# A sparse attention layer on one core: where the residual rows of the last tiles are put in order, who adds their output bias, and how the last projections are spread

## The chip, the cores and the metric

The kernel runs on one core of a Trainium2 chip. The metric is the device time of one launch in microseconds; before the change it is 2045.74 us, the median of three runs from 2043.18 to 2046.87. The profiled execution took 2043.34 us and has a span of 2041.5 us from its first to its last instruction. Times inside a trace count from the start of that span.

## The reference

One layer of attention over a graph, with a residual and a normalisation, in float32. x is 16 x 1024 x 512, adj a 1024 x 1024 matrix of zeros and ones shared by all batches and heads; there are 8 heads of 64.

```python
q = (x @ Wq + bq).reshape(b, n, H, HD)          # k and v alike
scores = jnp.einsum('bqhd,bkhd->bhqk', q, k) / jnp.sqrt(jnp.float32(HD))
scores = scores + (1.0 - adj)[None, None, :, :] * -1000000000.0
attn = jax.nn.softmax(scores, axis=-1)
out = jnp.einsum('bhqk,bkhd->bqhd', attn, v).reshape(b, n, d) @ Wo + bo
y = x + out
y = (y - mean(y)) / sqrt(var(y) + 1e-5)          # over the last axis
```

The random adj has few ones in a row (about four in the mean, many in the first rows and few in the last), so nearly all scores are masked.

## The kernel before, in words

The kernel computes scores for existing edges alone. It first counts the ones of each row of adj, sorts the 1024 queries by that count (`ranks`), and writes lists of edges (`edges`, L412): for tile t of 128 sorted queries, OWN[t] rounds in which each query meets one key of its own, and for the two densest tiles BLOCKS[t] further rounds in which a query with many keys takes several rows. A round is called a block: 35 per batch, 560 in all. `asked_row` holds the sorted order of the queries; whatever belongs to a sorted tile (its q rows, its residual rows of x, its output rows) is gathered or scattered by an indirect DMA on GpSimd (POOL) with it.

*Fronts.* For each batch and each pair of tiles of x, `pair` (L564) transposes x and multiplies by Wq, Wk and Wv (for k and v of two tiles together it uses a scheme with seven half products, L666). q, k and v go to DRAM rows by plain DMAs on the SP queue, and so does the row of the mean of v (L615), after which the batch counts as `set_up`. All of a batch's rows must be there before its blocks are gathered. The temporary tiles of this scheme are t1 to t4, e, w and g.

*Blocks.* For block n, `gather` (L788) fetches kv rows (L810), and where needed q rows (L794, L804); `products` (L827, DVE) and `scores` (L831, DVE) give the scores, `exponentials` (L841, ACT) their exponentials, `weigh` multiplies v (eight ACT instructions at L851, or DVE at L855), `add_own` (L867, DVE) or `add_up` (L876, L877, PE) sums. At the end of a tile `normalise` (L879) divides, PE transposes the result (L902) and ACT copies it (L906).

*Finish.* `load_y` (L719) gathers the tile's residual rows of x; `finish` (L736) multiplies by Wo (PE, four products of 512 columns, each two weight loads and two matmuls in the trace) and then, one or two loop steps apart: DVE adds the residual (L743) and the bias with a running sum (L744); DVE centres (L747); ACT squares (L751); DVE finishes the variance (L754); POOL takes the power -1/2 (L757); DVE makes the shift (L760); ACT normalises (L763); POOL scatters the rows to the output (L767).

The order of all this is written out by hand: one Python loop (L982 to L1053) over steps n from -34 (LEAD_IN) until all is done lays the instructions down, and each engine executes its own in that order. Step n works at different depths on different blocks: it lays products for block n + 4, exponentials for n + 3, sums for n, and gathers up to block n + 8, or n + 11 once no front is left. `later(k, fn)` lays something k steps further on, `later_last` does so at the end of that step. The lists are built by generators that advance once per step, from step -18 on (EDGES_FROM). On PE each step may spend a `share` of time, in which a product counts 0.86 (PRODUCT), four transposes 0.44 (TRANSPOSE), a sum 0.87 (SUM):

- in the lead-in (n < 0) 3.45 per step (LEAD_SHARE);
- for n from 0, set anew every 35 steps so that the fronts keep a fixed distance ahead of the blocks (EARLY = 13 blocks, and FIRST = 9 more in the first batch);
- from the end of batch 12 on, what is left of the fronts divided by the steps up to `fronts_end`, L977: (16 - 1) x 35 - 13 - 3 = 509;
- after the last front 3.0 (LAST_SHARE).

Tiles 102 to 111 (SPILL; tile 8 b + t) don't finish at once: their attention results go to DRAM and come back (`reload`, L730) once no front is left, to give PE work in the last stretch. Their residual rows are loaded into the temporaries t1 to t4 of the fronts, those of all other tiles into six buffers named y. At the end `guard` sets a flag that selects a general path for other inputs (`tile_general`); it isn't run here.

Of the kernel before, what the change touches and what calls it, by code (L numbers as in the profile page):

```python
# [32 lines left out]
LAZY = 2  # L33

SPILL = range(102, 112)
AHEAD_LAST = 11

ROWS = 3
EARLY = 13

FIRST = 9
LEAD_IN = 34
EDGES_FROM = (-17, -16, -15, -13, -11, -8, -7, -18)

# [1 line left out]
SUM = 0.87  # L46
TRANSPOSE = 0.44
LEAD_SHARE = 3.45
LAST_SHARE = 3.0

P = 128
# [103 lines left out]
def kernel(  # L155
# [66 lines left out]
    with ExitStack() as main:  # L222
# [49 lines left out]
        out_views = dram_disjoint_views(out, B * NT)  # L272
        x_rows = x.rearrange("b n d -> (b n) d")
        spill = [dram.tile([P, D], F32, name=f"spill_{i}") for i in range(len(SPILL))]
        zero = work.tile([1, D], F32, tag="q", name="zero", bufs=2)
        nc.gpsimd.memset(zero, 0.0)
        bias_rows = one.tile([2 * NPAIR, P], F32, name="bias_rows")
# [62 lines left out]
        def later(k, fn):  # L340
            plan.setdefault(now[0] + k, []).append(fn)
# [374 lines left out]

        loaded = {}

        def load_y(b, t, k=None):  # L719
            if k is None:  # L720
                Y[b, t] = work.tile([P, D], F32, tag="y", name=f"y_{b}_{t}", bufs=Y_BUFS)
            else:
                Y[b, t] = work.tile([P, 2, D], F32, tag=f"t{k % 4 + 1}", name=f"y_{b}_{t}", bufs=1)[:, 0, :]
            loaded[b, t] = now[0]
            nc.gpsimd.indirect_dma_start(  # L725
                out=Y[b, t], out_offset=None, in_=x_rows,
                in_offset=bass.IndirectOffsetOnAxis(ap=asked_row[:, t:t + 1], axis=0), element_offset=b * N * D,
            )

        def reload(b, t, k):  # L730
            OT[b, t] = work.tile([P, D], F32, tag="ewg"[k % 3], name=f"oTs_{b}_{t}", bufs=1)
# [3 lines left out]

        def finish(b, t):  # L736

            def out(p):
                OT.pop((b, t))
                y = Y[b, t]  # L740

                st = small.tile([P, 5], F32, name="stats", bufs=6)
                nc.vector.tensor_tensor(y, p, y, op=OP.add)  # L743
                nc.vector.scalar_tensor_tensor(y, bo_bc, 1.0, y, op0=OP.mult, op1=OP.add, accum_out=st[:, 0:1])  # L744

                def centre():
                    nc.vector.tensor_scalar(st[:, 1:2], st[:, 0:1], -1.0 / D, None, op0=OP.mult)  # L747

                def spread():
                    sq = work.tile([P, D], F32, tag="ysq", name=f"ysq_{b}_{t}", bufs=1)  # L750
                    nc.scalar.activation(sq, y, AF.Square, bias=st[:, 1:2], accum_out=st[:, 2:3])  # L751

                def variance():
                    nc.vector.tensor_scalar(st[:, 2:3], st[:, 2:3], 1.0 / D, EPS, op0=OP.mult, op1=OP.add)  # L754

                def power():
                    nc.gpsimd.tensor_tensor(st[:, 3:4], st[:, 2:3], neg_half, op=OP.pow)  # L757

                def shift():
                    nc.vector.tensor_tensor(st[:, 4:5], st[:, 3:4], st[:, 1:2], op=OP.mult)  # L760

                def norm_out():
                    nc.scalar.activation(y, y, AF.Identity, bias=st[:, 4:5], scale=st[:, 3:4])  # L763
                    later(2, store)

                def store():
                    nc.gpsimd.indirect_dma_start(  # L767
                        out=out_rows[b, t], out_offset=bass.IndirectOffsetOnAxis(ap=asked_row[:, t:t + 1], axis=0),
                        in_=y, in_offset=None, element_offset=b * N * D,
                    )  # L770
                    del Y[b, t]

                later(1, centre)
                later_last(2, spread)
                later(3, variance)
                later(4, power)
                later(5, shift)
                later_last(6, norm_out)

            return product(f"po_{b}_{t}", lambda: OT[b, t], W["o"], out)  # L780

# [184 lines left out]
        with tc.manual_schedule():  # L968

            fronts += transpose_x(0, 0) + transpose_x(0, 1)  # L970
            for b in range(B):
                for j in range(NT // 2):
                    fronts += pair(b, j)
            fronts_time = sum(u[0] for u in fronts)
            batch_time = fronts_time / B
            finishing, last_finish, reloads, last_reload = [], -LEAD_IN, 0, 0
            fronts_end = (B - 1) * NB - EARLY - 3  # L977
            credit = 0.0
            for t in range(3):
                load_x(0, t)  # L980
            n = -LEAD_IN
            while n < total or plan or rest or urgent or done or finishing or spilled:  # L982
                now[0] = n
                if n < 0:
                    share = LEAD_SHARE if n > -LEAD_IN else TRANSPOSE * 1.5
                elif n >= SPILL[0] // NT * NB + NB:

                    share = sum(u[0] for u in fronts) / max(fronts_end - n, 1) + NS * SUM / NB if fronts else LAST_SHARE
                elif n % NB == 0:

                    left = sum(u[0] for u in fronts)
                    goal = fronts_time - (n // NB + 2 + (EARLY + (FIRST if n < NB else 0)) / NB) * batch_time
                    share = (max(0.0, left - goal) + NT * NPAIR * PRODUCT + NS * SUM) / NB
                if 0 <= n + 3 < total:
                    exponentials(n + 3)
                if 0 <= n + 4 < total:
                    products(n + 4)
                while gathered[0] < min(n + (AHEAD if fronts else AHEAD_LAST) + 1, total) and blocks[gathered[0]][0] in set_up:
                    gather(gathered[0])
                    gathered[0] += 1  # L1000
                if 0 <= n + 1 < total and not by_act(n + 1):
                    weigh(n + 1)
                if 0 <= n < total and blocks[n][2] < OWN[blocks[n][1]]:
                    add_own(n)
                if 0 <= n + 4 < total:
                    scores(n + 4)
                if 1 <= n <= total and (n == total or blocks[n][2] == 0):
                    normalise(*blocks[n - 1][:2])
                for fn in plan.pop(n, ()):
                    fn()  # L1010
                if 0 <= n + 2 < total and by_act(n + 2):
                    weigh(n + 2)
                for fn in rest.pop(n, ()):
                    fn()
                credit += share
                if 0 <= n < total and blocks[n][2] >= OWN[blocks[n][1]]:
                    add_up(n)
                    credit -= SUM
                for tile_done in done[:0 if fronts and len(done) < LAZY else 1 if fronts else 2] + coming:
                    if tile_done not in loaded and sum(b * NT + t not in SPILL for b, t in Y) < 5:  # L1020
                        load_y(*tile_done)
                coming[:] = [t for t in coming if t not in loaded]
                if spilled and not fronts and n > last_reload + 2 and sum(b * NT + t in SPILL for b, t in Y) < 3:
                    reload(*spilled.pop(0), reloads)
                    reloads, last_reload = reloads + 1, n
                first_unit = True
                while credit > 0 or urgent:
                    if urgent and not (first_unit and fronts):
                        urgent.pop(0)()
                        continue  # L1030
                    if not finishing and len(done) > (LAZY if fronts else 0) and n > loaded.get(done[0], n) + 1 and n > last_finish + 1:
                        finishing = finish(*done.pop(0))
                        last_finish = n
                    units = finishing or fronts
                    if not units:
                        if urgent:
                            urgent.pop(0)()
                            continue
                        break
                    cost, fn, ready = units[0]  # L1040
                    if ready and not ready():
                        if urgent:
                            urgent.pop(0)()
                            continue
                        break
                    del units[0]
                    fn()
                    credit -= cost
                    first_unit = False
                credit = min(credit, share)  # L1050
                preps += prep.pop(n, [])
                preps = [g for g in preps if next(g, True) is None]
                n += 1  # L1053

    word = nc.values_load(  # L1055
# [32 lines left out]
```

## Time and profile before

| engine | busy us of the span | share |
|---|---|---|
| PE (TensorE) | 1917.2 | 94% |
| DVE (VectorE) | 1801.0 | 88% |
| ACT (ScalarE) | 1684.6 | 83% |
| POOL (GpSimd) | 1302.5 | 64% |

Three quarters of the DMA time belongs to the queue of indirect DMAs that POOL issues: 59.8% of the time of 16 DMA engines, against 18.4% for the plain transfers of SP. Three groups of indirect DMAs have one instruction per tile: the output rows (L767, 128 times, 1180 ns of POOL each), the residual rows (L725, 128 times, 1117 ns) and the q rows (L794, 128 times, 1097 ns); the kv rows (L810) have 560.

How to read it: a busy share over the whole span is a mean over stages with different limits. The page's second part cuts the span in 40 slices of 51 us, one digit of tenths each, and shows where an engine is full. A view of windows gives the same for chosen stretches in microseconds, with the clock granted to PE. A group line gives a source line, the engine, what it writes and reads, how often, busy time and mean duration, and after the second bar the engine's idle time just before these instructions with what ended it; "issue" there means that no other engine was waited for. PE's matmuls overlap in the records, so the spacing of its weight loads (PEld) tells its pace better than its busy time.

### The profile page before, as it was taken

The page shows a single profiled execution, that of the slowest core. Times are in us where ns is not written, and L with a number is a line of the kernel's source. Part 1 is how long each engine was busy: PE and PEld are TensorE (multiplying, and loading weights), DVE is VectorE, ACT ScalarE, POOL GpSimd, SP SyncE. Part 2 cuts the span into 40 slices and gives each one's busy share as a digit, 9 for nine tenths or more (in the row PEclk, how much of TensorE's full clock was granted, in tenths as well). Part 3 has the DMA queues.
Part 4 walks back from the last instruction along what each step waited for, and adds up shares of the span by engine and source line. Part 5 has one row for each costly group of instructions (what it writes and reads, how often), then busy time and mean ns, then how long its engine had stood idle before and what let it go on. Part 6 is the DMA issues. An engine that isn't in the chain of part 4 may idle for free. (4 is left out here: it accounts for less than half of the span.)

```text
span 2041.5 us, 26505 instructions
## 1 busy us (share of the span) xinstructions
PE 1917.2 (94%) x5334; PEld 925.4 (45%) x5334; DVE 1801.0 (88%) x3675; ACT 1684.6 (83%) x7048; POOL 1302.5 (64%) x1224
## 2 busy tenths in 40 slices
PE   8979999899999999999999999999999999997565
PEld 4434454444545444444544444454544444443232
DVE  3798889889999989989999999989999999997684
ACT  4627879888897988889897989879798889987684
POOL 1432557757576666757676676758677675757884
PEclk9999999999999999999999999999999999999897
DMA  6565787878888787878888797888888799978773
GB/s 244 154 202 195 241 297 264 296 237 303 288 295 292 261 307 258 310 242 303 293 287 307 242 327 250 293 283 289 293 271 305 257 321 313 326 255 281 231 253 103
DMA packets 183657, 549.50 MB, mean 269 GB/s; under 512 B 30879, under 2 KB 30907, under 8 KB 183486
## 3 DMA queue, kind: packets, MB, share of 16 engines
q0 software_dynamic: 121632, 403.22, 59.8%
q1 hardware_dynamic: 59248, 139.53, 18.4%
q10 hardware_dynamic: 2606, 4.99, 0.7%
q14 instruction: 127, 1.04, 0.2%
q8 instruction: 44, 0.72, 0.1%
HBM read 435.44 MB, written 136.89 MB: 280 GB/s over the span
## 5 line engine op out<-in xcount | busy, mean ns | idle before, releaser
L810 POOL DMA_INDIRECT kvg<-kv_rows,key_row x560 | 634.9, 1134 | 468.1 <-ACT pv L841 145.1
L851 ACT ACTIVATE pv<-kvg,pv 128x64 f32<-128x64 f32 x3608 | 910.2, 342 | 0.0
L550 PE MATMUL pq<-wq,xT 128*128 128x512 f32 x1024 | 479.7, 599 | 0.2 <-DVE g L685 0.2
L550 PE MATMUL po<-wo,oT 128*128 128x512 f32 x944 | 439.0, 599 | 0.7 <-ACT oT L906 0.7
L831 DVE TENSOR_REDUCE s<-qk 128x8 f32<-128x512 f32 x560 | 381.0, 680 | 6.4
L827 DVE TENSOR_TENSOR qk<-qt,kvg 128x512 f32<-128x512 f32 x464 | 317.4, 684 | 5.9 <-DMA kvg<-kv_rows,key_row 5.8
L550 PEld LDWEIGHTS pq<-wq,xT 128*128 128x128 f32 x1024 | 193.8, 192 | 216.2 <-issue 197.4
L550 PEld LDWEIGHTS po<-wo,oT 128*128 128x128 f32 x944 | 176.5, 192 | 209.2 <-issue 191.8
L666 PE MATMUL x<-b,xT 128*128 128x512 f32 x504 | 239.1, 597 | 0.0
L666 PE MATMUL pp<-t,s 128*128 128x512 f32 x504 | 237.0, 592 | 0.4 <-DVE s L536 0.4
L867 DVE TENSOR_TENSOR pv<-pv,pv 128x520 f32<-128x520 f32 x336 | 233.1, 694 | 0.2 <-ACT pv L851 0.2
L841 ACT ACTIVATE pv<-s,absent 128x8 f32<-128x8 f32 x464 | 136.9, 296 | 85.1 <-DVE s L831 55.8
L767 POOL DMA_INDIRECT out_dram<-y,asked_row x128 | 151.0, 1180 | 35.5 <-issue 16.9
L725 POOL DMA_INDIRECT y<-in_x_dram,asked_row x128 | 143.0, 1117 | 38.9 <-issue 37.7
L562 ACT ACTIVATE sq<-q 128x128 f32<-128x128 f32 x512 | 151.1, 303 | 17.5 <-DVE q L577 17.1
L794 POOL DMA_INDIRECT qt<-q_rows,asked_row x128 | 140.4, 1097 | 38.9 <-issue 34.6
L562 ACT ACTIVATE sq<-kv 128x128 f32<-128x128 f32 x512 | 151.0, 302 | 0.1
L666 PEld LDWEIGHTS x<-b,xT 128*128 128x128 f32 x504 | 95.8, 191 | 116.6 <-issue 111.5
L666 PEld LDWEIGHTS pp<-t,s 128*128 128x128 f32 x504 | 94.8, 190 | 110.6 <-issue 99.2
L902 PE MATMUL poT<-ident,o 128*128 128x128 f32 x512 | 79.5, 279 | 50.2 <-DVE o L894 34.1
L666 PE MATMUL z<-b,s 128*128 128x512 f32 x252 | 120.1, 599 | 5.0 <-DVE kv L694 5.0
L804 POOL DMA_INDIRECT qg<-q_rows,query_row x96 | 106.9, 1114 | 27.8 <-issue 24.1
(168 smaller groups left out, 2816.1 us busy)
## 6 DMA issues: line engine op xcount, KB each, us to landing
kv_rows<-kv SPq DMA_DIRECT2D x128, 512.0 KB
x<-in_x_dram SPq DMA_DIRECT2D x128, 256.0 KB
q_rows<-q SPq DMA_DIRECT2D x128, 256.0 KB
kvg<-kv_rows,key_row POOLq DMA_INDIRECT x560, 5.8
adj<-in_adj_dram POOLq DMA_DIRECT2D x8, 512.0 KB, 12.7
spill<-oT SPq DMA_DIRECT2D x10, 256.0 KB
oTs<-spill SPq DMA_DIRECT2D x10, 256.0 KB
qt<-q_rows,asked_row POOLq DMA_INDIRECT x128, 5.0
```

The lines of the kernel that those rows point to most:

```text
L550: nc.tensor.matmul(p, lhs()[:, ts(c, P)], w[:, c, :], start=(c == 0), stop=(c == NPAIR - 1))
L562: nc.scalar.activation(sq, s[:, ts(h, P)], AF.Square, accum_out=NRM[b][:, i, t, h:h + 1])
L666: nc.tensor.matmul(R[bank], l[:, ts(c, P)], right[:, c, :], start=(first and c == 0), stop=(c == 1), skip_group_check=True,)
L725: nc.gpsimd.indirect_dma_start(out=Y[b, t], out_offset=None, in_=x_rows, in_offset=bass.IndirectOffsetOnAxis(ap=asked_row[:, t:t + 1], axi ...
L767: nc.gpsimd.indirect_dma_start(out=out_rows[b, t], out_offset=bass.IndirectOffsetOnAxis(ap=asked_row[:, t:t + 1], axis=0), in_=y, in_offse ...
L794: nc.gpsimd.indirect_dma_start(out=QT[b, t], out_offset=None, in_=q_rows[b % ROWS], in_offset=bass.IndirectOffsetOnAxis(ap=asked_row[:, t: ...
L810: nc.gpsimd.indirect_dma_start(out=KG[n], out_offset=None, in_=kv_rows[b % ROWS], in_offset=bass.IndirectOffsetOnAxis(ap=key_row[:, g:g + ...
L827: nc.vector.tensor_tensor(QK[n], q, KG[n][:, 0:D], op=OP.mult)
L831: nc.vector.tensor_reduce(S[n], QK.pop(n).rearrange("p (h d) -> p h d", d=HD), axis=AX.X, op=OP.add)
L841: nc.scalar.activation(PV[n][:, D:], S.pop(n), AF.Exp, bias=bias)
L851: nc.scalar.activation(pv[:, ts(h, HD)], v[:, ds(D + h * HD, HD)], AF.Copy, scale=pv[:, D + h:D + h + 1])
L867: nc.vector.tensor_tensor(PV[b, t], PV[b, t], pv, op=OP.add)
```

## The change

It does three things.

1. *Residual put in order early.* While the lists are built (steps -16 to -4, SORTED_AT, two tiles a step), POOL gathers the residual rows of the last 26 tiles (102 to 127) and SP writes them to DRAM in sorted order (`sort_residual`). When such a tile finishes, `load_y` takes it by a plain DMA on SP in place of an indirect one on POOL. It takes 26 indirect DMAs out of POOL's queue near the end.
2. *Bias on PE.* For tiles whose finish starts after the last front, the output bias is added in PSUM by one more product (a column of the identity, broadcast, times `bo_bc`), so that DVE's first addition falls away and the second takes PSUM and residual together. The shift and what follows it move one step later for these tiles.
3. *Fronts spread otherwise.* In the lead-in the share from step -16 on is 4.6 in place of 3.45 (LISTS_SHARE); in the first batch the fronts run 11 in place of 9 blocks further ahead (FIRST); and the last front is due at step (16 - 1) x 35 - 12 = 513 in place of 509, nearer to the blocks of the last batch, which need it.

```diff
--- before.py
+++ after.py
@@ -33,12 +33,14 @@
 LAZY = 2
 
 SPILL = range(102, 112)
+
+SORTED_AT = range(-16, -3)
 AHEAD_LAST = 11
 
 ROWS = 3
 EARLY = 13
 
-FIRST = 9
+FIRST = 11
 LEAD_IN = 34
 EDGES_FROM = (-17, -16, -15, -13, -11, -8, -7, -18)
 
@@ -46,6 +48,7 @@
 SUM = 0.87
 TRANSPOSE = 0.44
 LEAD_SHARE = 3.45
+LISTS_SHARE = 4.6
 LAST_SHARE = 3.0
 
 P = 128
@@ -272,6 +275,7 @@
         out_views = dram_disjoint_views(out, B * NT)
         x_rows = x.rearrange("b n d -> (b n) d")
         spill = [dram.tile([P, D], F32, name=f"spill_{i}") for i in range(len(SPILL))]
+        residual = [dram.tile([P, D], F32, name=f"residual_{i}") for i in range(B * NT - SPILL[0])]
         zero = work.tile([1, D], F32, tag="q", name="zero", bufs=2)
         nc.gpsimd.memset(zero, 0.0)
         bias_rows = one.tile([2 * NPAIR, P], F32, name="bias_rows")
@@ -716,16 +720,27 @@
 
         loaded = {}
 
+        def gather_x(y, b, t):
+            nc.gpsimd.indirect_dma_start(
+                out=y, out_offset=None, in_=x_rows,
+                in_offset=bass.IndirectOffsetOnAxis(ap=asked_row[:, t:t + 1], axis=0), element_offset=b * N * D,
+            )
+
+        def sort_residual(i):
+            y = work.tile([P, D], F32, tag="y", name=f"y_sorted_{i}", bufs=Y_BUFS)
+            gather_x(y, *divmod(SPILL[0] + i, NT))
+            later(2, lambda: nc.sync.dma_start(residual[i], y))
+
         def load_y(b, t, k=None):
             if k is None:
                 Y[b, t] = work.tile([P, D], F32, tag="y", name=f"y_{b}_{t}", bufs=Y_BUFS)
             else:
                 Y[b, t] = work.tile([P, 2, D], F32, tag=f"t{k % 4 + 1}", name=f"y_{b}_{t}", bufs=1)[:, 0, :]
             loaded[b, t] = now[0]
-            nc.gpsimd.indirect_dma_start(
-                out=Y[b, t], out_offset=None, in_=x_rows,
-                in_offset=bass.IndirectOffsetOnAxis(ap=asked_row[:, t:t + 1], axis=0), element_offset=b * N * D,
-            )
+            if b * NT + t >= SPILL[0]:
+                nc.sync.dma_start(Y[b, t], residual[b * NT + t - SPILL[0]])
+            else:
+                gather_x(Y[b, t], b, t)
 
         def reload(b, t, k):
             OT[b, t] = work.tile([P, D], F32, tag="ewg"[k % 3], name=f"oTs_{b}_{t}", bufs=1)
@@ -735,13 +750,19 @@
 
         def finish(b, t):
 
+
+            biased = not fronts
+
             def out(p):
                 OT.pop((b, t))
                 y = Y[b, t]
 
                 st = small.tile([P, 5], F32, name="stats", bufs=6)
-                nc.vector.tensor_tensor(y, p, y, op=OP.add)
-                nc.vector.scalar_tensor_tensor(y, bo_bc, 1.0, y, op0=OP.mult, op1=OP.add, accum_out=st[:, 0:1])
+                if not biased:
+                    nc.vector.tensor_tensor(y, p, y, op=OP.add)
+                nc.vector.scalar_tensor_tensor(
+                    y, p if biased else bo_bc, 1.0, y, op0=OP.mult, op1=OP.add, accum_out=st[:, 0:1]
+                )
 
                 def centre():
                     nc.vector.tensor_scalar(st[:, 1:2], st[:, 0:1], -1.0 / D, None, op0=OP.mult)
@@ -774,10 +795,19 @@
                 later_last(2, spread)
                 later(3, variance)
                 later(4, power)
-                later(5, shift)
-                later_last(6, norm_out)
-
-            return product(f"po_{b}_{t}", lambda: OT[b, t], W["o"], out)
+                k = 5 if fronts else 6
+                later(k, shift)
+                later_last(k + 1, norm_out)
+
+            units = product(f"po_{b}_{t}", lambda: OT[b, t], W["o"], out)
+            if biased:
+                def bias():
+                    nc.tensor.matmul(
+                        PS[f"po_{b}_{t}"], ident[:, 0:1].to_broadcast([P, P]), bo_bc, start=False, stop=False
+                    )
+
+                units.insert(2, (PRODUCT, bias, None))
+            return units
 
 
 
@@ -974,7 +1004,7 @@
             fronts_time = sum(u[0] for u in fronts)
             batch_time = fronts_time / B
             finishing, last_finish, reloads, last_reload = [], -LEAD_IN, 0, 0
-            fronts_end = (B - 1) * NB - EARLY - 3
+            fronts_end = (B - 1) * NB - 12
             credit = 0.0
             for t in range(3):
                 load_x(0, t)
@@ -982,7 +1012,7 @@
             while n < total or plan or rest or urgent or done or finishing or spilled:
                 now[0] = n
                 if n < 0:
-                    share = LEAD_SHARE if n > -LEAD_IN else TRANSPOSE * 1.5
+                    share = LISTS_SHARE if n > -16 else LEAD_SHARE if n > -LEAD_IN else TRANSPOSE * 1.5
                 elif n >= SPILL[0] // NT * NB + NB:
 
                     share = sum(u[0] for u in fronts) / max(fronts_end - n, 1) + NS * SUM / NB if fronts else LAST_SHARE
@@ -1050,6 +1080,9 @@
                 credit = min(credit, share)
                 preps += prep.pop(n, [])
                 preps = [g for g in preps if next(g, True) is None]
+                if n in SORTED_AT:
+                    for i in range(2):
+                        sort_residual(2 * (n - SORTED_AT[0]) + i)
                 n += 1
 
     word = nc.values_load(
```

## The prediction

> **What bounds the kernel now.** I read the page first, its second part (the span in 40 slices of 51 us), for where the engines change places:
>
> ```profile
> PE   8979999899999999999999999999999999997565
> DVE  3798889889999989989999999989999999997684
> POOL 1432557757576666757676676758677675757884
> PEclk9999999999999999999999999999999999999897
> ```
>
> There are three regimes: a beginning where PE has gaps, a long middle with PE full, and three to four slices at the end where PE falls to half and POOL rises to its highest. To cut them exactly I need times for the steps n of the kernel's loop. The trace has one L827 product per block, laid at step n = block - 4, and the front products (pq, L638, L666) in order on PE. With the order of both built programs this puts PE's step 0 at 160 us, step 35 at 299, 455 at 1685, 490 at 1781 and 509, where the fronts run out, at 1849 (the last L666 matmul is there). The view of windows, cut so (columns: PE, weight loads, DVE, ACT, POOL busy, then clock and DMA):
>
> ```profile
> 80.00:160.00 80.00, 63.50 (x158) 28.45 (x157) 76.03 (x149) 27.15 (x121) 22.77 (x23) 0.93 0.57 186
> 160.00:299.00 139.00, 137.01 (x382) 66.09 (x382) 118.49 (x245) 113.02 (x503) 71.15 (x65) 0.98 0.74 248
> 520.00:1570.00 1050.00, 1048.78 (x2973) 509.96 (x2972) 973.44 (x1974) 924.49 (x3924) 715.80 (x657) 1.00 0.83 285
> 1849.00:2017.00 168.00, 110.20 (x265) 53.09 (x264) 127.22 (x306) 124.65 (x450) 132.22 (x135) 0.85 0.72 237
> 2017.00:2041.50 24.50, 6.20 (x14) 2.48 (x13) 3.50 (x11) 2.91 (x5) 4.52 (x5) 0.70 0.16 57
> ```
>
> From 80 to 160 (the lists) DVE is busy 95%. In the middle PE is: weight loads of a product lie 0.43 us apart and a product has two, so it costs 0.86 us; a batch of 79.3 us of fronts, 32 output products, 6 sums and 8 transposes of 0.44 us is 115.6 us, against 116.6 us from batch to batch. From 1849 to 2017 POOL is busy only 132 of 168 us, but its groups there say that the rest is no wait for others:
>
> ```profile
> L810 POOL DMA_INDIRECT kvg<-kv_rows,key_row x40 | 45.2, 1129 | 14.1 <-issue 11.1 <-ACT pv L851 2.1 <-DMA out_dram<-y,asked_row 0.3
> L767 POOL DMA_INDIRECT out_dram<-y,asked_row x23 | 24.9, 1080 | 4.8 <-issue 4.0 <-ACT pv L841 0.5 <-ACT y L763 0.2
> L725 POOL DMA_INDIRECT y<-in_x_dram,asked_row x21 | 22.9, 1091 | 6.4 <-issue 5.8 <-PE poT L902 0.3 <-DMA qg<-q_rows,query_row 0.3
> L757 POOL TENSOR_TENSOR stats<-stats,neg_half 128x1 f32<-128x1 f32 x24 | 16.4, 683 | 5.4 <-DVE stats L747 4.9
> ```
>
> Each indirect DMA has about 0.3 us of "issue" before it: 1.4 us for a residual row gather, (22.9+6.4)/21. And the waits of that stretch name who waits for POOL:
>
> ```profile
> DVE stats L760 <- POOL stats L757: 33.6, 14, 8.1
> ACT y L763 <- DVE stats L760: 12.0, 6, 6.0
> ```
>
> So the last stretch is bound by POOL's queue; the power L757 is queued behind gathers, and DVE and then ACT stand behind the power. After 2017 comes one chain for the last tile, 24.5 us.
>
> **What the Trainium skill says.** "DMA: Bandwidth & Descriptors", SWDGE vs HWDGE vs iDMA: a GpSimd DMA's descriptors are computed by software on GpSimd, those of SP by hardware. The trace agrees on POOL's side: 1.09 us of POOL per gather. The same page, Issuing engines are not separate DMA queues: all run on the same 16 engines, another issuer saves issue time alone. The last stretch has a DMA share of 0.72, so issue time is what is missing there. "Perfetto Trace Analysis", Optimization Strategy: regimes with different bounds are to be interleaved; the change moves POOL work to where POOL is busy 22.8 of 80 us. "TensorE: Matmul & The Clock Gate", HAM oscillation: idle gaps over about 3.4 us lower PE's clock. The trace agrees: 0.85 in the last stretch (waits of PE up to 14.2 us on DVE o L894), 1.00 in the middle.
>
> **The change part by part.**
>
> Residual in order. 22 of the 26 gathers were laid from step 509 on (21 before 2017); they leave POOL, 21 x 1.4 = 29 us, and become plain loads on SP. SP is idle there; its loads need a y buffer whose store was laid four or more steps earlier, so I cost them at nothing. Queued behind such a load on SP are the spilled oT, and early in the stretch q_rows, kv_rows and the mean row of the last batch, for which POOL's first gather of that batch waits.
>
> Their price in the lead-in: 26 gathers, 36 us of POOL, two at each step from -16 to -4, where POOL is idle 57 of 80 us. A gather waits for one of six y buffers, which the SP write of three steps before frees; behind it on POOL stand gathers of codes and the first kvg, for which DVE's list work waits. Codes are used three steps (over 10 us) after their gather, so nothing is lost at the low end. At the high end DMA decides: 26 x 0.52 MB = 13.6 MB in some 65 us is 210 GB/s on top of 186, and the busiest 10 us of the trace moved 408. I take 2 us, 0 to 12.
>
> More fronts early (LISTS_SHARE, FIRST). By step 0 the fronts done go from 114.5 to 132.1 us of PE, 17.6 more, or 1.8 tiles. The lead-in is DVE's: a tile costs q, 2.5 sums of w, g, k and v, two narrow sums at 0.42 and one vsum, the wide ones with starts 0.60 us apart, 3.4 us; so +6 us. Step 0 to 35 then has 117.2 us of PE work in place of 131.4; at the old ratio (139/131.4, less a little) 123 us, so -16. DVE would have 118.5 - 5 us there and stays below. By step 70 both versions have done the same fronts; 35 to 70 was above its PE work (98 for 82 us), DVE-bound, and gives -1, 70 to 105 -1. Sum with the sort: -10 us. It is PE idle time of the lead-in put to use.
>
> Last fronts later (fronts_end 509 to 513). Steps 455 to 490 have 84 us of PE work in place of 90, but DVE is busy 94 of 96 us there: -2. Steps 490 to 513 have 76.2 in place of 65.4 us, at 68/65.4: +11 us. The four steps are bought at 2.8 us each and leave a stretch in which each cost 168/51 = 3.3. The fronts end about where they did, -1: 1848 us.
>
> Last stretch, now 47 steps. POOL: 168 - 29 (residual) - 5.8 (4 kvg) - 1.4 (1 qg) - 4.1 (3 stores) = 128 us. DVE: 127 - 21 x 0.6 (the sum L743) - 4 x 2.2 = 106. ACT: 125 - 10 = 115. PE: 90 us of work grows by 21 products for the bias (18 us) and loses some 4: 104 at full clock, 122 at 0.85. The trace has no product with a broadcast stationary; by the nearest row (po, two weight loads) it is 0.86 us, and 1.0 at the low clock; I take 0.86. The bias saves DVE a 0.6 us sum and its wait for nothing else; PE has room. POOL stays the bound. To it I add 5 us where its first gather of the last batch waits for the mean row, which is laid only at step 516 with that gather at 517 (this wait took 5.9 us in the lead-in), and 2 us for waits among four engines now within 22 us of each other. The later shift (k + 1) costs nothing: it gives POOL one step more to deliver the power. 135 us.
>
> Last chain: one product more (0.86 to 1.0), one sum less (0.69): 24.7 us.
>
> Sum: 1848 + 135 + 25 = 2008 us of span, 33.5 below 2041.5. The time lies 4.2 us above the span of the profile, so 2012.
>
> **The rivals.** (a) The bound passes on: PE with bias products at 0.85, or the mutual waits of DVE, ACT, POOL and PE, hold the stretch at 150 us: 2027. For it: PE at 122 and POOL at 128 are close, and the order ties DVE to POOL within two steps. Against: in the middle PE 100%, DVE 93% and ACT 88% run side by side with 1% lost; and a busier PE keeps its clock. (b) The lead-in pays: DMA near its limit delays codes and rows by 12 to 15 us, the tail gains as above: 2024. (c) Slower: the sort lies wholly on the path (each gather behind a buffer that SP frees late, lists and first gathers behind it), 36 us, and the earlier fronts then gain nothing (+10): 2012 + 36 - 2 + 10 = 2056. For it: POOL and SP queues are in order, and DVE has no slack in the lead-in. Against: 57 us of idle POOL, and codes three steps ahead.
>
> **How the numbers follow.** Forecast 0.64, (a) 0.18, (b) 0.11, (c) 0.07. The low end takes the stretch at POOL's bare 126 us and the lead-in at no cost: 2000, a little less if PE fills steps 0 to 35 without loss: 1998. The high end takes in (a) and most of (b): 2029. Faster by over 0.2% 0.91, same 0.02, slower 0.07.
>
> **What would show it.** POOL: no L725-like gather in the last stretch, its busy share still the highest there, and the wait of the shift for the power well below 33.6 us. Step 0 near 167 us, step 35 near 290, fronts' end near 1848, 135 us from there to the last block, 25 after it. Wrong if DVE has idle time between 80 and 170 us behind codes or kvg, if PE heads the last stretch, or if waits for y loads on SP appear before L744.

## The result, and the profile after

The changed kernel takes 2012.89 us (median; 2011.79 to 2013.06), the kernel before beside it 2044.53 us (2043.18 to 2046.87): ratio 0.9843, 95% interval 0.9826 to 0.9860. The span of the profiled execution went from 2041.5 to 2011.1 us. The forecast was 2012 us. That it is met within 1 us is luck: several of its terms were wrong, in opposite directions, which is what the experiments are about.

The page after, its second part (40 slices, now of 50 us):

```profile
PE   8988998899999999999999999999999999899885
DVE  3799999899899998989899898999999998999784
POOL 1673657767576675767667575767767575566784
PEclk9999999999999999999999999999999999999898
```

PE's last slices read 9, 8, 9, 9, 8, 8, 5 where they read 9, 9, 9, 7, 5, 6, 5, and POOL has new work in its second and third slices. By the rule that the prediction used (front products on PE against the order of the program) PE's step 0 is at 169.3 us, step 35 at 290, 70 at 394, 455 at 1681, 490 at 1778; the last front (now due at 513) ends at 1858.4, and the last block's sums are read by DVE at 1986.0. Lines of the changed kernel have other numbers than before: L840, L788 and L778 are the gather of kv rows, the scatter of output rows and the power, which were L810, L767 and L757; L763 and L781 are the residual with the running sum and the shift, which were L744 and L760. The view of windows of the changed kernel, cut there (PE, weight loads, DVE, ACT, POOL busy, clock, DMA share, GB/s):

```profile
80.00:160.00 80.00, 71.56 (x183) 31.61 (x182) 74.09 (x138) 29.91 (x141) 53.58 (x48) 1.00 0.98 354
169.00:290.00 121.00, 121.00 (x346) 59.49 (x346) 111.84 (x234) 102.91 (x452) 66.43 (x63) 0.98 0.80 265
290.00:394.00 104.00, 88.00 (x237) 41.19 (x236) 93.28 (x190) 92.92 (x384) 77.28 (x71) 0.95 0.81 268
514.00:1566.00 1052.00, 1048.32 (x2971) 509.39 (x2970) 971.38 (x1971) 924.17 (x3924) 709.98 (x658) 1.00 0.83 284
1858.00:1986.00 128.00, 112.00 (x295) 53.60 (x294) 103.07 (x260) 108.46 (x396) 97.52 (x102) 0.95 0.81 281
1986.00:2011.00 25.00, 6.82 (x14) 2.88 (x14) 3.05 (x13) 4.33 (x8) 4.15 (x5) 0.70 0.10 35
```

The last stretch takes 128 us in place of 168 and the fronts end 9 us later: 40 - 9 - 1 (last chain) = 30 us of span. In that stretch POOL's groups no longer hold a gather of residual rows, and DVE's wait for the power is down from 33.6 us to 10.5. POOL's groups there, then the waits:

```profile
L840 POOL DMA_INDIRECT kvg<-kv_rows,key_row x36 | 40.7, 1131 | 14.1 <-issue 7.5 <-DMA kv_rows<-mean 4.0 <-ACT pv L881 0.8
L788 POOL DMA_INDIRECT out_dram<-y,asked_row x22 | 24.5, 1113 | 5.9 <-issue 2.7 <-ACT pv L871 1.1 <-ACT y L784 0.8
L778 POOL TENSOR_TENSOR stats<-stats,neg_half 128x1 f32<-128x1 f32 x21 | 14.5, 692 | 5.1 <-DVE stats L768 2.9 <-DVE stats L775 1.2 <-DVE stats L781 0.6
```

```profile
ACT pv L871 <- DVE s L861: 11.4, 12, 2.4
DVE stats L781 <- POOL stats L778: 10.5, 9, 2.2
DVE y L763 <- PE po L554: 9.5, 5, 3.9
PE poT L932 <- DVE o L924: 7.9, 4, 3.0
POOL kvg L840 <- DMA kv_rows<-mean: 4.0, 1, 4.0
```

Of the gaps before POOL's instructions, 4.0 us are the wait for the mean row and 4.7 us waits for DVE at the power; without these POOL has about 119 of the 128 us, counting the short gap before each of its instructions. The other waits go round: ACT for DVE, DVE for POOL and for PE, PE for DVE, 8 to 11 us each. The forecast had put the wait for the mean row at 5 us.

### The profile page after: what moved, and what is told of

The parts are those of the page before. It is cut to its first block, busy times and chain, and to the rows that moved or that the text cites. A ratio compares the mean times of both kernels' runs of the same rounds, so it can differ in the third digit from the quotient of the medians.

```text
span 2011.1 us, 26727 instructions
## 1 busy us (share of the span) xinstructions
PE 1923.4 (96%) x5378; PEld 926.2 (46%) x5378; DVE 1785.5 (89%) x3653; ACT 1682.9 (84%) x7048; POOL 1303.5 (65%) x1224
## 5 line engine op out<-in xcount | busy, mean ns | idle before, releaser
L840 POOL DMA_INDIRECT kvg<-kv_rows,key_row x560 | 635.8, 1135 | 453.5 <-ACT pv L871 142.9
L861 DVE TENSOR_REDUCE s<-qk 128x8 f32<-128x512 f32 x560 | 381.5, 681 | 6.8 <-DVE qk L857 0.5
L788 POOL DMA_INDIRECT out_dram<-y,asked_row x128 | 153.3, 1198 | 36.0 <-issue 16.3
L724 POOL DMA_INDIRECT y<-in_x_dram,asked_row x102 | 115.5, 1132 | 30.0 <-issue 27.8
L670 PE MATMUL z<-t,s 128*128 128x512 f32 x252 | 120.0, 599 | 0.0
```

Source lines behind the costliest of these rows:

```text
L670: nc.tensor.matmul(R[bank], l[:, ts(c, P)], right[:, c, :], start=(first and c == 0), stop=(c == 1), skip_group_check=True,)
L724: nc.gpsimd.indirect_dma_start(out=y, out_offset=None, in_=x_rows, in_offset=bass.IndirectOffsetOnAxis(ap=asked_row[:, t:t + 1], axis=0), ...
L788: nc.gpsimd.indirect_dma_start(out=out_rows[b, t], out_offset=bass.IndirectOffsetOnAxis(ap=asked_row[:, t:t + 1], axis=0), in_=y, in_offse ...
L840: nc.gpsimd.indirect_dma_start(out=KG[n], out_offset=None, in_=kv_rows[b % ROWS], in_offset=bass.IndirectOffsetOnAxis(ap=key_row[:, g:g + ...
L861: nc.vector.tensor_reduce(S[n], QK.pop(n).rearrange("p (h d) -> p h d", d=HD), axis=AX.X, op=OP.add)
```

## The experiments

Three groups of four kernels ran on one chip each, with the kernel before beside them. It took 2048.47 us beside the first group (the sort undone, the sort alone, the plain rows, the first kernel with the bias back on DVE), 2043.31 beside the second (the bias product alone, the changed kernel again, the fronts' end at 509, the early fronts undone) and 2054.62 beside the third (the rest). So timed values are compared by their ratio to it; an expected time in us belongs to a kernel before of about 2045 us. From the traces I take two things: the time from the end of the last front to the read of the last block's sums, called the stretch, and the times of given blocks' products on DVE.

**The sort undone**

```diff
-            if b * NT + t >= SPILL[0]:
-                nc.sync.dma_start(Y[b, t], residual[b * NT + t - SPILL[0]])
-            else:
-                gather_x(Y[b, t], b, t)
+            gather_x(Y[b, t], b, t)
...
-                if n in SORTED_AT:
-                    for i in range(2):
-                        sort_residual(2 * (n - SORTED_AT[0]) + i)
```

> The changed kernel with the residual sort undone: all residual rows gathered by POOL when they are needed, nothing sorted in the lead-in; bias product, early fronts and later fronts' end stay. My theory (POOL's queue bounds the last stretch, and the 22 gathers taken out of it are the gain): the stretch from the end of the fronts to the last block goes from 128 to about 155 us (21 x 1.4 us more, less the 4 us wait for the mean row), the lead-in gets 0 to 2 us shorter: 2036 to 2041 us. Rival (the bias product or the spread of the fronts brings the gain): 2013 to 2018 us.

Measured: 2041.09 us, ratio 0.9962 (0.9948 to 0.9976), against 0.9843 with the sort: 1.2%, 24 us, of the 1.6% hang on it. The stretch is 152.4 us long. POOL's groups in it:

```profile
L723 POOL DMA_INDIRECT y<-in_x_dram,asked_row x21 | 22.1, 1050 | 6.3 <-issue 6.0 <-PE po L553 0.3
```

These 21 gathers hold (22.1 + 6.3) = 28.4 us of POOL, and the stretch is 24.8 us longer than with the sort. So POOL's queue did bound it, as the theory said; the rival that gave the gain to the bias or the fronts falls.

**The sort alone**

```diff
-FIRST = 11
+FIRST = 9
...
-LISTS_SHARE = 4.6
+LISTS_SHARE = 3.45
...
-            biased = not fronts
+            biased = False
...
-                k = 5 if fronts else 6
+                k = 5
...
-            fronts_end = (B - 1) * NB - 12
+            fronts_end = (B - 1) * NB - EARLY - 3
```

> The kernel before with the residual sort alone: bias on DVE, fronts spread as before, shift not moved. My theory: 21 gathers leave POOL in the last stretch (168 us, 51 steps), 139 us then, DVE 127 and ACT 125 beside it; lead-in 0 to 2 us longer: 2016 to 2022 us. Rival (without the bias on PE another engine holds the stretch): DVE and waits keep it at 155 us or more, 2032 us or above.

Measured: 2027.39 us, ratio 0.9895 (0.9878 to 0.9911); by the ratio that is 2023 us beside a kernel before of 2044.5, just over my range and well under the rival's. The stretch is 147.1 us, where I expected 139. The view of windows, and POOL's power in it:

```profile
1857.00:2004.00 147.00, 109.43 (x265) 51.67 (x263) 126.92 (x306) 122.40 (x448) 114.94 (x114) 0.86 0.79 269
L778 POOL TENSOR_TENSOR stats<-stats,neg_half 128x1 f32<-128x1 f32 x24 | 19.8, 825 | 8.8 <-DVE stats L768 8.4
```

The gathers taken out (29 us) gave 21 us. Of the missing 8 us, 3.5 are at the power, which waits 8.4 us for DVE (4.9 before), and 3.4 are the power itself, 825 ns each where it took 683; why it takes longer isn't shown. The wait was the first sign that DVE's work, and with it the bias, matters.

**What the sort costs in the lead-in**

```diff
-                nc.sync.dma_start(Y[b, t], residual[b * NT + t - SPILL[0]])
+                nc.sync.dma_start(Y[b, t], x[b, ds(t * P, P), :])
...
-                        sort_residual(2 * (n - SORTED_AT[0]) + i)
```

> The changed kernel without the sort, with the last 26 tiles' residual loaded by the same plain SP loads from x itself, so that these tiles add rows in unsorted order: it leaves out the ordering of the residual alone. It prices the 26 gathers and 26 writes of the lead-in. My theory: they cost 0 to 2 us, so 2011 to 2013 us. Rival (the lead-in pays for the DMA traffic and the queue, 5 us or more): 2008 us or below.

Measured: 2013.11 us, ratio 0.9823 (0.9807 to 0.9840); the changed kernel has 0.9843. The difference, 4 us, has the width of the intervals: by its own time this kernel is where the theory put it, by the ratio (2008 us) where the rival did. In the traces the sort can't be seen on the path: block 0's product on DVE comes at 143.5 us without it, at 145.4 and 143.2 in two profiles with it, and the stretch is 131.9 us without it, no shorter than with it. The window 80 to 160 without the sort

```profile
80.00:160.00 80.00, 71.86 (x184) 31.72 (x183) 75.15 (x145) 31.48 (x148) 22.03 (x20) 1.00 0.58 197
```

has the same PE, DVE and ACT time as with it (above); POOL has 32 us less and the DMA engines are at 0.58 in place of 0.98. A lead-in with the DMA engines busy 0.98 of the time cost little here; what it carried was wanted only 1700 us later.

This kernel is a second test of the main claim. It and the kernel without the sort have the same lead-in and differ in the queue that brings the last residual rows, SP's or POOL's: the stretch is 131.9 us against 152.4, the ratio 0.9823 against 0.9962.

**The bias back on DVE**

```diff
-            biased = not fronts
+            biased = False
```

> The changed kernel with the bias added by DVE again for all tiles; sort and spread of the fronts stay. My theory: DVE has 13 us more in the last stretch, 119 us, still under POOL's 129, and PE 18 us less: 2013 us, give or take 3. Rival (DVE's relief is needed once POOL is relieved): DVE's extra work comes on top, 2020 to 2026 us. Second rival (PE is the tight engine after the change): faster, 2004 to 2009 us.

> The changed kernel with the bias on DVE, again, with more rounds. The first look had 10 us more in the last stretch, the timed runs 0.2% with an interval that reaches zero. If DVE's relief is worth something once POOL is relieved: 0.986 to 0.989 of the kernel before (2016 to 2021 us). If the first look was chance: 0.984 (2012 us).

Measured: 2022.08 us, ratio 0.9863 (0.9842 to 0.9883), and again 2032.73 us, ratio 0.9887 (0.9861 to 0.9912), against 0.9843 and 0.9844 (below) with the bias product. The first interval takes in 0.9843, so the timing alone would leave it open. Both traces agree on the stretch: 137.6 and 138.8 us, where three traces with the same program there (the changed kernel twice, and the one with the early fronts undone) have 127.6, 128.6 and 128.4. It is the same program up to step 513, so the 10 us belong to this edit. My theory, that nothing changes, fell. The stretch of the second kernel in the view of windows, and of the first the waits that grew:

```profile
1870.00:2009.00 139.00, 100.96 (x253) 48.29 (x251) 117.48 (x281) 109.36 (x399) 102.50 (x102) 0.88 0.76 258
```

```profile
PEld poT L932 <- DVE o L924: 11.2, 3, 5.9
PE poT L932 <- ACT pv L881: 10.2, 2, 8.2
PE sum L906 <- DVE pv L885: 9.1, 3, 5.0
L778 POOL TENSOR_TENSOR stats<-stats,neg_half 128x1 f32<-128x1 f32 x21 | 16.0, 761 | 10.4 <-DVE stats L768 4.7 <-DVE stats L775 4.0 <-DVE stats L781 1.3
```

DVE is busy 117 us, well below 139. PE now waits for DVE and ACT in pieces of up to 8 us, and DVE waits for the products of the outputs (8.5 us at L762). POOL's queue isn't what it was either: its power waits 10 us for DVE in place of 4.7, and the same 102 instructions take 102.5 us in place of 97.5. These two together are about as long as the 10 us. A sum of one engine's work doesn't give this length. Two things stay open: why POOL's instructions take longer, and how much PE's clock, 0.88 in place of 0.95 with less work on PE, adds; no run separates DVE's work from that clock. The later shift stays in this kernel, so its own worth isn't measured.

**The bias product alone**

```diff
-FIRST = 11
+FIRST = 9
...
-LISTS_SHARE = 4.6
+LISTS_SHARE = 3.45
...
-            if b * NT + t >= SPILL[0]:
-                nc.sync.dma_start(Y[b, t], residual[b * NT + t - SPILL[0]])
-            else:
-                gather_x(Y[b, t], b, t)
+            gather_x(Y[b, t], b, t)
...
-            fronts_end = (B - 1) * NB - 12
+            fronts_end = (B - 1) * NB - EARLY - 3
...
-                if n in SORTED_AT:
...
```

> The kernel before with the bias product and the later shift alone. My theory (POOL bounds the last stretch, 168 us; DVE and PE have room): no change, within 3 us of the kernel before. Rival (DVE's relief shortens the stretch by itself, as the 10 us between the changed kernel with and without the bias product suggest): 6 to 10 us faster.

Measured: 2043.40 us, ratio 1.0004 (0.9993 to 1.0014). Here the theory holds. The stretch is 166.9 us:

```profile
1848.00:2015.00 167.00, 128.77 (x309) 61.74 (x307) 112.41 (x283) 122.96 (x447) 133.13 (x134) 0.87 0.73 236
```

DVE has 112 us in place of 127 and PE 129 in place of 110, and neither moves the end, since POOL has its 133 us and the gaps before its instructions. The same edit is worth nothing while POOL is the bound and 10 us of the stretch once it is relieved.

**Two products for the bias**

```diff
-                    nc.tensor.matmul(
...
+                    for _ in range(2):
+                        nc.tensor.matmul(
...
-                units.insert(2, (PRODUCT, bias, None))
+                units.insert(2, (2 * PRODUCT, bias, None))
```

> The changed kernel with the bias product made twice for each of the 22 tiles (they add the bias twice, so the output is off by the bias, which is zero in these inputs). It adds 19 us of PE work to the last stretch and nothing else. If PE has room there, as the prediction had it (104 us of work at full clock), the stretch grows by 4 us at most: 2012 to 2016 us. If PE is next to the bound (rival a), most of the 19 us arrives: 2022 us or more.

Measured: 2026.64 us, ratio 0.9882 (0.9856 to 0.9908). By the ratio (2020 us) the time is between what the two readings expected; the trace tells more. The stretch is 132.8 us, 5 more than with one product, with 15 us more of PE in it:

```profile
1867.00:2000.00 133.00, 127.17 (x336) 60.42 (x335) 103.17 (x262) 108.37 (x393) 97.97 (x102) 0.97 0.79 271
```

So PE had room for about three quarters of the 19 us, and the stretch is then PE's (127 of 133). The rest of the slower time lies before step 513, where this program is the same as the changed kernel (its fronts end at 1867.0 us, 8.6 later), so it doesn't come from the edit.

**The fronts' end back at 509, and the changed kernel beside it**

```diff
-            fronts_end = (B - 1) * NB - 12
+            fronts_end = (B - 1) * NB - EARLY - 3
```

> The changed kernel as it is, again, to be compared with the other three on one chip: 0.984 of the kernel before, 2012 us where the kernel before has 2045.

> The changed kernel with the last front due at step 509 again. Theory from the traces: after the change the last stretch costs 2.7 us a step (128 us for 47 steps), and the steps with fronts cost about 3 us each at the margin (the fronts end 9 us later for four steps more), so the four steps are worth the same on either side: 2012 us, give or take 3. Rival (the later end is needed, since the last stretch is POOL's): 4 x 3.3 us come back and only 9 us are won, or PE's spare work in the last stretch is missing: 2016 us or more.

Measured: the changed kernel 2011.55 us, ratio 0.9844 (0.9830 to 0.9857); with 509 2016.33 us, ratio 0.9860 (0.9845 to 0.9876). In the traces the fronts end at 1856.2 and 1846.0 us and the stretch takes 128.6 and 144.5: the four steps cost 10.2 us before the fronts' end and save 15.9 after it. Timed, it is 3 to 5 us with intervals that overlap; the sign is that of the rival.

**The early fronts undone**

```diff
-FIRST = 11
+FIRST = 9
...
-LISTS_SHARE = 4.6
+LISTS_SHARE = 3.45
```

> The changed kernel with the share of fronts in the lead-in and in the first batch as before (3.45, 9). Prediction's size: 12 us slower, 2024 us. Theory from the traces: only half of it arrived, the blocks of the second batch are reached 4 to 6 us earlier than before: 2017 us. Rival (the fronts' earlier start is taken back later altogether): 2012 us.

Measured: 2016.96 us, ratio 0.9876 (0.9857 to 0.9894), 0.3% or 5 to 7 us over the changed kernel on the same chip. The products on DVE tell where it goes (without, with): block 0 at 138.1 and 143.2 us, 35 at 279.1 and 272.1, 70 at 387.3 and 381.5, 140 at 620.0 and 613.3, 420 at 1553.4 and 1547.7. The lead-in pays 5, the first batch gives 12, nothing more comes after that: 6 to 7 us net, half of what the prediction had.

**The power left out**

```diff
-                    nc.gpsimd.tensor_tensor(st[:, 3:4], st[:, 2:3], neg_half, op=OP.pow)
+                    nc.vector.tensor_copy(st[:, 3:4], st[:, 2:3])
```

> The changed kernel with the power -1/2 left out on POOL (a DVE copy of the variance stands in its place, so the output is scaled wrongly: the square root of the normalisation is left out). It takes 21 x 0.95 us of POOL out of the last stretch and with it DVE's wait for POOL. If POOL's queue still bounds the stretch after the change, it goes from 128 to about 112 to 116 us, where ACT (107 us) and PE (112 us) stand: 1997 to 2001 us where the changed kernel has 2012. If the stretch is already held by the waits among PE, ACT and DVE, it stays within 4 us: 2008 us or more.

Measured: 2065.79 us, ratio 1.0040 (1.0018 to 1.0061), slower than the kernel before, which neither reading expected. It can't be read as meant: the edit reaches all 128 tiles, and blocks 140 to 420 took 960.8 us in place of 934.4, long before the stretch. The stretch itself took 138.9 us with POOL waiting for ACT, and DVE for something outside the program:

```profile
POOL out_dram L788 <- ACT pv L871: 21.1, 7, 5.7
POOL kvg L840 <- DMA kv_rows<-mean: 7.6, 1, 7.6
DVE y L763 <- remote: 6.8, 1, 6.8
```

("remote" is a wait that nothing in the program's records ended; there are 71 us of them over the engines here, 12 to 30 us in the three others on that chip, 6 to 35 us in the four of the first group, none in the profiles of the changed kernel.) Why the middle slowed stays open, and with it how much more POOL's relief would bring.

**Fronts further ahead in all batches**

```diff
-ROWS = 3
-EARLY = 13
-FIRST = 11
+ROWS = 4
+EARLY = 20
+FIRST = 4
```

> The changed kernel with fronts 20 blocks ahead in all batches (EARLY 20, FIRST 4, and four instead of three sets of q and kv rows in DRAM, without which the order isn't allowed). The second batch's steps have 16 us of idle PE in the changed kernel, since the extra distance of the first batch is taken back there; here they do 16 us more of the fronts, which leaves 11 us less for the steps 455 to 490 (held by DVE there, so 0 to 2 us gained) and 7 us less for the steps 490 to 513 (PE-bound, 7 us gained). Theory: 2003 to 2007 us. Rival (DVE, busy 93 of 104 us in the second batch, can't take it): 2011 us or more.

Measured: 2030.77 us, ratio 0.9898 (0.9871 to 0.9924), against 0.9887 for the kernel with the bias on DVE and 0.9882 for the one with two products on that chip. The second batch takes the fronts as meant:

```profile
290.00:394.00 104.00, 98.29 (x276) 47.16 (x275) 94.84 (x196) 97.47 (x416) 75.81 (x70) 0.98 0.83 276
```

PE is busy 98 of 104 us in place of 88. But nothing of it is left: blocks 105 to 420 take 1071 us, against 1058 and 1061 in the two programs beside it that are equal to the changed kernel there. What slows them isn't settled. So the rival's range (2011 us or more) was right, though its reason isn't shown. No version with correct rows measured here beats the changed kernel.

## Why the prediction was right, and where it wasn't

**What bounds the last stretch: right.** The step "21 x 1.4 = 29 us" leave POOL is shown by the kernel without the sort: 28.4 us of POOL, 24.8 us of the stretch, 24 us of the time. That is three quarters of the whole gain.

**The length of the stretch: 128 us measured, 135 forecast.** Most of the 7 us lies in the waits. The forecast's "168 - 29 ... = 128" for POOL isn't work alone. Busy time and all gaps together give the length of a stretch for any engine, so that the 168 us are filled proves nothing by itself; the kernel without the sort does. Some 7 us of POOL's gaps before were waits for DVE and ACT (4.9 at the power, 2.1 at a gather), so "the rest is no wait for others" was a little too strong. The forecast thus had 121 us of POOL's own and 14 of waits (these 7, 5 for the mean row, 2 among the engines); measured are 119 and 9. The smaller work fits the counts: of kv gathers 36 were left, as forecast, but 6 gathers of q rows (qg) in place of 9 and 21 powers in place of 24, against 22 stores in place of 20.

**The bias: wrong.** "The bias saves DVE a 0.6 us sum and its wait for nothing else" costed it at no gain. It holds for the kernel before (1.0004), not for the kernel it was applied in: there it is 10 us of the stretch. The step compared DVE's sum of work (106, or 119 with the sums) with POOL's (128) and took the larger; measured, 117 us of DVE beside POOL made 138 us. A sum takes 0.68 us in the trace, and the waits that it causes were put at nothing. Since the forecast took the bias as given in its total, the total wasn't hurt.

**Rival (a): half right.** It held that the bound passes on and that PE or mutual waits keep 150 us. A sign that the forecast named against itself is there: PE heads the stretch now (112 us busy), and POOL's share, 97.5 us, isn't "still the highest" but the lowest of the four. Waits of DVE for PE (9.5 us) stand before L763; the other sign, waits for the residual loads there, doesn't appear. The bound did become shared: 19 us more of PE work cost 5 us, 14 us of DVE work cost 10. But the stretch isn't 150 us. PE's clock was 0.95 there in place of 0.85, with PE busy 88% of it in place of 66%, which is the way the forecast argued against the rival.

**The early fronts: right in kind, half in size.** Step 0 came at +9 us (forecast +8), step 35 at -9 (forecast -8), both on PE. The step that failed is "35 to 70 ... DVE-bound, and gives -1": it took 104 us in place of 98. The kernel before:

```profile
299.00:397.00 98.00, 87.03 (x242) 40.99 (x241) 91.04 (x188) 89.36 (x372) 70.30 (x68) 0.98 0.83 277
```

DVE has the most work there in both kernels (91 and 93 us), and its products tell what was passed on: they were 6.6 us early at block 35, not the 9 of PE's step, and 4.7 at block 70. The forecast's -10 for all that the lead-in gives became -4 by step 455.

**The last fronts: right in kind, with the same debt.** From 490 to the fronts' end 80.6 us (forecast 79). The "-2" for steps 455 to 490 was +0.5; DVE was the limit there, as stated, and gave nothing. So the fronts ended at 1858 us, not 1848: of the 10 us, 6 come from the lead-in and the first batches, 2.5 from these steps and 1.5 from the last 23. The 10 us too many here and the 7 too few in the stretch left 3 us of span.

**The last step of the sum: luck.** The forecast added 4.2 us from span to time. That was the median time less the span of one execution, which itself took only 1.8 us more than its span; in the changed kernel it is 1.8 us again. These 2.4 us too many offset most of the 3 us too few, and so the forecast of 2012 stands beside 2012.89.

**The sort's price: within its range, at the low end.** 2 us forecast, 0 to 12 allowed; the traces show none, the timed ratio 4 us with an interval that takes in none. Rivals (b) and (c) fall: the gathers waited for their buffers 4.6 us in all.

```profile
L724 POOL DMA_INDIRECT y_sorted<-in_x_dram,asked_row x26 | 29.5, 1136 | 11.4 <-issue 6.7 <-DMA residual<-y_sorted 4.6
```

## What to carry to other kernels

An engine can bound a stretch with a busy share of 79% (132 of 168 us) when each of its instructions has a short gap of its own before it, here about 0.3 us: add the gaps named "issue" to the busy time before asking who is full, and leave out the waits for others. Work that depends on nothing late, here the residual rows, can be done in a stage where its engine and the DMA engines have room, even at the price of a trip through DRAM. And once the bound is relieved, don't take the next engine's sum for the new length: here four engines had 98 to 112 us of busy time each, and an edit that was worth nothing before (a sum of 0.68 us per tile) was worth 10 us, so measure parts both alone and in place.

## What the runs showed of the hardware that I had not expected

DMA engines busy 0.98 of the lead-in (354 GB/s, 13.6 MB more than before) delayed nothing that could be seen in the times of the first products. The product with a broadcast column as its stationary took 607 ns per matmul in the records of the stretch; those with a full tile took 592 and 630 there:

```profile
L805 PE MATMUL po<-bo_bc,ident 128*128 128x512 f32 x42 | 22.0, 607 | 0.0
```

And the same program, with the bias back on DVE, took 934 us from block 140 to block 420 on one chip and 944 on another; so only lengths of a stage and ratios to the kernel before on the same chip are compared here.
